# Transposes in place of identity products in a gather that runs beside a recurrent convolution

## The chip, the core and the metric

The kernel runs on one core of a Trainium2 chip. The core has engines that run side by side, each with its own queue of instructions that it works off in order: PE (TensorE, matrix products; its weight loads are listed apart as PEld), DVE (VectorE), ACT (ScalarE) and POOL (GpSimd). SP issues most of the DMAs, POOL the gathers. PE writes to PSUM[...] and the other engines read its results there. The metric is the device time in microseconds (us) of one execution; the median of several runs is given.

## The reference

The input is `x`, 8 images of 128 channels by 64 x 64 points, in fp32. Four layers follow each other, and each adds to its input what it computes from a group-normalized copy (`_gn`). Layer 0 is a selective state-space scan beside a small convolution. Layer 1 is a recurrence: four sweeps over the image (down, up, right, left), in each of which a line becomes itself plus the ReLU of a nine-tap convolution of the line before:

```
def step(prev, cur):
    new = cur + jax.nn.relu(_conv1d(prev, w))
    return (new, new)
```

Layer 2 multiplies a vertical convolution by grouped sums. Layer 3 is a deformable convolution. From an ordinary convolution it takes, for each point and each of nine taps, a position and a mask; it fetches the four corners of the input around the position, sums them with bilinear weights, and multiplies the nine sums by `dcn_w`:

```
samp = corner(y0, x0, ...) + corner(y0, x0 + 1, ...) + corner(y0 + 1, x0, ...) + corner(y0 + 1, x0 + 1, ...)
samp = samp * mask[:, None]
out = jnp.einsum('bckhw,ock->bohw', samp, dcn_w.reshape(COUT, C, KK))
```

A normalization over the batch, gamma and beta, and a leaky ReLU end it.

## The kernel before

Layer 1 works on four images at once, which lie in the tile `X`. Its first four images run beside Layer 0 (`Layer1First`). Its second four run in the main loop of `conv_preact_kernel`, beside Layer 2 and Layer 3 of the first images. The change concerns this main loop.

The loop counts ticks `n`, 96 to an image. In each tick it records, in this order: one step of Layer 1 if one is due (`next(step)`, line 130), which puts the nine products of a line into `ps_l` (L733); the tick of Layer 3 (`three.tick`, line 132) for the image before the one that Layer 2 works on; then the second half of Layer 1's step (line 134), a vector operation that adds the ReLU of `ps_l` to the line in `X` (L741); then what Layer 2's plan has for that tick. The plan (`Layer2.plan`) gives each of its parts a tick by hand: convolution products into `ps_t` (L894, L908), normalization, token transposes that fill the gather tables (`tokens`, L966, which turns 128 x 128 blocks of `x3h` into `ps_tok` by `nc.tensor.transpose`), offset products into `ps_off` (L990), and the positions, masks and weights of the corners on the vector engine (L1023 to L1052). The order in which instructions are recorded is the order in which each engine works; there is no scheduler that would move them. The next step's products need the line that L741 has just written, so PE may have to wait there; what was recorded between the two fills that time.

A tick of Layer 3 handles 128 points and three of the nine taps (`gather`). POOL issues three indirect DMAs (L1123), one per tap, that bring for each point the four corners (four rows of 128 channels) into `got`, or, from tick 402 on, into a part of `X`, which is free by then. `got` has six buffers. The corners 2 and 3 are weighted on ACT (L1134), the corners 0 and 1 on DVE (L1139, into `prod`). What follows depends on `halves`. Line 132 passes 1 while `n < L1Z`, which is 362, and 2 after that. With `halves == 2`, one vector addition (L1141) leaves two partial sums in `got`, and PE adds them. With `halves == 1`, as long as Layer 1 runs, DVE adds all four corners (L1143 to L1145) and leaves one sum, in `got[:, k, 0, :]`.

The sums have points on partitions and channels along the row; the convolution needs channels on partitions. So one tick later `turn` lets PE turn them: for each of the three taps a product with `got` as the stationary operand and the identity as the moving one goes into a third of the PSUM tile `ps_s` (L1155), and with two halves a second product accumulates onto it. Another tick later ACT copies `ps_s` to `samp` (L1106, where `later` calls it), and for each two blocks of points `convolve` multiplies by `dcn_w` into `ps_o` (L1166). `ps_s` has two buffers. `later` runs its calls from `tick`, after that tick's `gather`.

Of the kernel before, what the change touches and what calls it, by code (L numbers as in the profile page):

```python
# [1085 lines left out]
class Layer3:  # L1086
# [63 lines left out]
    def turn(self, halves, got, samp, col):  # L1150
        nc = self.nc
        ps = self.pp.tile([P, self.G3, P], F32, name="ps_s")
        for k in range(self.G3):
            for q in range(halves):
                nc.tensor.matmul(  # L1155
                    ps[:, k, :], lhsT=got[:, k, q, :], rhs=self.ident, start=(q == 0), stop=(q == halves - 1)
                )
        self.later(1, nc.scalar.copy, samp[:, :, col : col + P], ps)

    def convolve(self, b, t0, k0, samp):  # L1160
# [118 lines left out]
```

## Time and profile before

| what | value |
|---|---|
| median of 3 runs | 7738.29 us (7735.23 to 7739.29) |
| the profiled execution | 7708.51 us |
| its span, first to last instruction | 7706.8 us |
| mean granted clock of PE | 0.903 |
| PE busy | 6228.2 us, 81% of the span |
| DVE, POOL, ACT busy | 4497.4, 4009.0, 3460.5 us |
| last product of Layer 1 | 5224 us after the span's start |

Busy time is the union of an engine's instructions. Matmuls are pipelined, so that the duration of one includes a latency that overlaps with the next, and the distance between starts says what one costs in a row of them. The granted clock is the share of full speed that the throttle allows PE. A wait is put down to the last of its releasers that the records name; "issue" and "another core or an unknown queue" stand for releasers that they do not name.

### The profile page before, as it was taken

Reading aid. Unit: us, or ns where it says so; the run is one execution under the profiler, and the core shown is the slowest. Engines: PE = TensorE matmul, PEld = TensorE weight load, DVE = VectorE, ACT = ScalarE, POOL = GpSimd, SP = SyncE. Lnnn points to the kernel's source line nnn. Section 1 sums busy time; section 2 is a strip of 40 time slices with the busy share of each in tenths; the row PEclk is TensorE's granted clock in tenths of the full one; section 3 lists DMA queues with packets and bytes.
Section 4 is the critical chain, followed back from the end, with each engine's and each line's share of the span. In section 5 each row is a group of like instructions: output and inputs, shape, how many; then the busy total and the mean of one; then the engine's idle time right before and its main releaser. Section 6 shows DMA issues by size and latency. Waiting matters only on the chain.

```text
span 7706.8 us, 87506 instructions
## 1 busy us (share of the span) xinstructions
PE 6228.2 (81%) x30574; PEld 4062.3 (53%) x30574; DVE 4497.4 (58%) x5332; ACT 3460.5 (45%) x8218; POOL 4009.0 (52%) x3261
## 2 busy tenths in 40 slices
PE   6888878799999999859898898986678777776661
PEld 1222222255555556637677777775555555555550
DVE  4888889666566566141265666657545454555445
ACT  4555656433333332020155445455455555555552
POOL 3767777444444444000155555456566666666664
PEclk9988889699999999979999999998889888988785
DMA  1011111000000000041255556567666666666667
GB/s 43 27 38 36 39 34 38 31 11 27 12 29 21 9 15 15 12 157 29 66 182 183 166 174 192 167 186 253 204 210 202 208 194 208 201 206 203 186 185 264
DMA packets 333017, 897.81 MB, mean 116 GB/s; under 512 B 55464, under 2 KB 90544, under 8 KB 330528
## 3 DMA queue, kind: packets, MB, share of 16 engines
q0 software_dynamic: 184320, 604.13, 26.0%
q1 hardware_dynamic: 143648, 271.31, 10.6%
q10 hardware_dynamic: 4608, 16.78, 0.5%
q8 instruction: 242, 3.96, 0.2%
q14 instruction: 199, 1.63, 0.1%
HBM read 770.80 MB, written 121.21 MB: 116 GB/s over the span
## 4 chain that ended last, share of the span: by engine, by line
PE 62%; ACT 12%; DVE 8%; issue 8%; another core or an unknown queue 5%; DMA 3%; POOL 2%; SPq 0%; DVEq 0%; POOLq 0%; ACTq 0%
PE u_ps L733 13%; PE ps_l L733 10%; PE ps_s L1155 8%; PE ps_o L1166 6%; PE u_ps L568 5%; ACT X L1134 4%; PE ps_c L477 3%; PE ps_t L894 3%; DVE hb L603 3%; PE ps_y L622 3%; PE ps_x L395 3%; PE ps_t L908 2%; ACT samp L1106 1%; PE ps_off L990 1%
## 5 line engine op out<-in xcount | busy, mean ns | idle before, releaser
L614 POOL TENSOR_TENSOR hb<-hb,bc 128x1024 f32<-128x1024 f32 x512 | 1217.2, 2385 | 1279.7 <-ACT carry L609 893.5
L1123 POOL DMA_INDIRECT X<-table,idx x1386 | 1315.4, 949 | 788.4 <-issue 304.4
L1123 POOL DMA_INDIRECT got<-table,idx x918 | 878.6, 957 | 1351.4 <-DVE idx L1046 545.9
L603 DVE TENSOR_TENSOR_SCAN hb<-da,carry,u_ps 128x512 f32<-128x512 f32 x896 | 1097.8, 1266 | 251.0 <-PE ps_y L622 178.5
L585 ACT ACTIVATE da<-dt_ps 128x1024 f32<-128x1024 f32 x512 | 524.3, 1024 | 1337.7 <-PE dt_ps L568 1337.0
L1155 PE MATMUL ps_s<-ident,X 128*128 128x128 f32 x5544 | 829.7, 308 | 268.0 <-issue 175.7
L1141 DVE TENSOR_TENSOR X<-prod,X 128x768 f32<-128x768 f32 x462 | 442.4, 958 | 916.7 <-ACT X L1134 706.6
L1155 PEld LDWEIGHTS ps_s<-ident,X 128*128 128x128 f32 x5544 | 794.6, 221 | 339.3 <-issue 212.2
L1134 ACT ACTIVATE X<-X,wgt 128x128 f32<-128x128 f32 x2772 | 860.5, 394 | 0.0
L1166 PE MATMUL ps_o<-samp,dcn_w 128*128 128x256 f32 x2304 | 646.3, 422 | 225.3 <-ACT samp L1106 140.5
L568 PE MATMUL u_ps<-u,m_u 32*128 32x512 f32 x2048 | 629.6, 693 | 152.7 <-DVE hb L603 152.5
L1106 ACT COPY samp<-ps_s 128x384 f32<-128x384 f32 x768 | 360.9, 470 | 796.7 <-remote 479.9
L592 DVE TENSOR_TENSOR u_ps<-u_ps,bc 128x1024 f32<-128x1024 f32 x512 | 624.7, 1220 | 153.8 <-PE dt_ps L568 136.9
L568 PE MATMUL dt_ps<-dt,m_dt 32*128 32x512 f32 x2048 | 631.6, 695 | 17.5 <-ACT da L585 17.4
L1166 PEld LDWEIGHTS ps_o<-samp,dcn_w 128*128 128x128 f32 x2304 | 464.6, 212 | 332.9 <-ACT samp L1106 159.6
L1134 ACT ACTIVATE got<-got,wgt 128x128 f32<-128x128 f32 x1836 | 569.5, 393 | 0.0
L1139 DVE TENSOR_TENSOR prod<-X,prod 128x768 f32<-128x768 f32 x462 | 443.6, 960 | 100.6 <-ACT prod L1113 47.1
L741 DVE SCALAR_TENSOR_TENSOR X<-ps_l,X 128x256 f32<-128x256 f32 x252 | 106.2, 421 | 620.3 <-PE ps_l L733 473.4
L568 PEld LDWEIGHTS u_ps<-u,m_u 32*128 32x128 f32 x2048 | 164.8, 196 | 510.0 <-DVE hb L603 311.1
L741 DVE SCALAR_TENSOR_TENSOR X<-u_ps,X 128x256 f32<-128x256 f32 x252 | 106.9, 424 | 501.7 <-PE u_ps L733 501.3
L894 PE MATMUL ps_t<-xn,w 128*128 128x512 f32 (+4 forms) x688 | 305.2, 592 | 54.8 <-ACT t L901 22.5
L1155 PE MATMUL ps_s<-ident,got 128*128 128x128 f32 x2076 | 294.0, 287 | 38.2 <-issue 28.6
(227 smaller groups left out, 10393.2 us busy)
## 6 DMA issues: line engine op xcount, KB each, us to landing
table<-tok SPq DMA_DIRECT2D x128, 256.0 KB
x<-x1d SPq DMA_DIRECT2D x96, 256.0 KB
X<-table,idx POOLq DMA_INDIRECT x1386
x<-x2d SPq DMA_DIRECT2D x48, 384.0 KB
x3h<-x3d SPq DMA_DIRECT2D x16, 1056.0 KB
x_st<-in_x SPq DMA_DIRECT2D x64, 256.0 KB
x_o<-in_x SPq DMA_DIRECT2D x64, 256.0 KB
x1d<-res SPq DMA_DIRECT2D x64, 256.0 KB
```

Of the source, the lines that this page charges most:

```text
L568: nc.tensor.matmul(ps[:, j, :], lhsT=mask[q, r].rearrange("p d n -> p (d n)"), rhs=S[c][src, h][q, :], start=True, stop=True,)
L585: nc.scalar.activation(da, steps[i]["dt"], AF.Exp)
L592: nc.vector.tensor_mul(st["bc"], st["bc"], s["bc", h][:, 0].unsqueeze(1).to_broadcast([P, 2, T]))
L603: nc.vector.tensor_tensor_scan(hb[:, j, :], st["da"][:, j, :], st["bc"][:, j, :], start, ALU.mult, ALU.add)
L614: nc.gpsimd.tensor_mul(hb, hb, S[c]["bc", h][:, 1].unsqueeze(1).to_broadcast([P, 2, T]))
L733: nc.tensor.matmul(ps[:, c0:c1, :], lhsT=w[:, k, :], rhs=v[:, prev, c0 + k - PAD : c1 + k - PAD, :], start=(k == PAD), stop=(k == K - 1),)
L894: nc.tensor.matmul(ps[:, o0 - a0 : o1 - a0, :], lhsT=self.w1[:, k, :], rhs=S["xn", g][:, i0 + o0 : i0 + o1, :], start=(k == 2), stop=(k == 4),
L1123: nc.gpsimd.indirect_dma_start(out=got[:, k, :, :].rearrange("p q c -> p (q c)"), out_offset=None, in_=tab, in_offset=bass.IndirectOffsetO ...
L1134: nc.scalar.activation(got[:, k, q, :], got[:, k, q, :], AF.Identity, scale=wgt[:, t, k0 + k, q : q + 1])
L1139: nc.vector.tensor_mul(prod, got[:, :, 0:2, :], w.unsqueeze(3).to_broadcast([P, G3, 2, C]))
L1155: nc.tensor.matmul(ps[:, k, :], lhsT=got[:, k, q, :], rhs=self.ident, start=(q == 0), stop=(q == halves - 1))
L1166: nc.tensor.matmul(ps, lhsT=self.dcn_w[:, k, :], rhs=samp[:, k - k0, :], start=(k == 0), stop=(k == KK - 1))
```

## The change

In `turn`, where one half is left, each tap's product with the identity is replaced by a PE transpose of the same tile, again with `got` stationary and the identity moving, into the same third of `ps_s`. Where two halves are left, the two accumulating products stay as they are. No other line is touched.

```diff
         for k in range(self.G3):
-            for q in range(halves):
-                nc.tensor.matmul(
-                    ps[:, k, :], lhsT=got[:, k, q, :], rhs=self.ident, start=(q == 0), stop=(q == halves - 1)
-                )
+            if halves == 1:
+                nc.tensor.transpose(ps[:, k, :], got[:, k, 0, :], self.ident)
+                continue
+            for q in range(2):
+                nc.tensor.matmul(ps[:, k, :], lhsT=got[:, k, q, :], rhs=self.ident, start=(q == 0), stop=(q == 1))
         self.later(1, nc.scalar.copy, samp[:, :, col : col + P], ps)
```

## The prediction

> **What bounds the kernel now.** I began with the page: its first part, and the row of the operation that the change touches.
>
> ```profile
> PE 6228.2 (81%) x30574; PEld 4062.3 (53%) x30574; DVE 4497.4 (58%) x5332; ACT 3460.5 (45%) x8218; POOL 4009.0 (52%) x3261
> L1155 PE MATMUL ps_s<-ident,got 128*128 128x128 f32 x2076 | 294.0, 287 | 38.2 <-issue 28.6
> ```
>
> TensorE is the busiest engine over the span, but an average over stages decides nothing. The row counts matmul instructions whose stationary tile is `got`. Line 1123 issues 918 gathers into `got`, three a tick, so 306 ticks. With a of them at `halves == 1`, 2076 = 6a + 12(306 - a) gives a = 266: a fp32 product is recorded as two instructions, six for the three products of a tick. The loop agrees: ticks 96 to 361. The other 40 use `got` with two halves; the 5544 rows on `X` are two halves too. By the starts of `ps_s`, the 266 ticks fill 3821 to 5228 us. The stages by windows (window; busy us and count of PE, PEld, DVE, ACT, POOL; granted clock, DMA share, GB/s):
>
> ```profile
> 3821.00:5228.00 1407.00, 1286.30 (x6549) 1061.21 (x6548) 867.85 (x1438) 709.97 (x2106) 753.09 (x793) 0.97 0.58 178
> 5228.00:5443.00 215.00, 146.67 (x705) 116.64 (x705) 159.96 (x220) 106.76 (x324) 127.09 (x128) 0.82 0.77 254
> 5443.00:7535.00 2092.00, 1482.99 (x8268) 1212.67 (x8267) 1030.70 (x1200) 1172.52 (x3572) 1296.50 (x1367) 0.85 0.65 198
> ```
>
> In the stage of the change PE is busy 91%, the next engine (DVE) 62%; only there does the diff alter an instruction. Then the chain of work that ended last, cut to that window, by line:
>
> ```profile
> by line: PE ps_l L733 36.7%; PE ps_o L1166 9.4%; PE ps_s L1155 8.0%; PE ps_t L894 7.1%; another core or an unknown queue 6.8%; issue 5.4%; PE ps_t L908 3.9%; ACT got L1134 3.4%; PE ps_off L990 2.8%; DVE prod L1139 2.4%; DMA got<-table,idx 1
> ```
>
> `ps_s` holds 8.0% of 1407 us, 113 us of the critical chain. Last, PE's own waits there (us in total, times, longest):
>
> ```profile
> PE ps_l L733 <- DVE X L741: 46.4, 20, 7.8
> PE ps_tok L966 <- ACT tok L969: 27.0, 22, 6.0
> PE ps_l L733 <- issue: 13.2, 9, 4.6
> PE gn_ps L750 <- DVE gn_mv L749: 8.3, 3, 4.1
> ```
>
> PE idles 1407 - 1286 = 121 us, mostly where layer 1's next step waits for the vector add of the last (L741). These waits take part of any gain.
>
> **What the skill says.** "TensorE: Matmul & The Clock Gate", Terms, says the load and the matmul gained a transpose mode on trn2, four times as fast for fp32. Part 4 of that page gives about 275 ns for one transpose in a kernel, and says that transposes do not count as busy for the clock gate. Part 1 says that the gate halves the clock after an idle window of about 3.4 us. The trace already has transposes of this very shape and type, at L966, so their price is measured here (groups of `ps_tok`, then of `ps_s`; ns min/median/max):
>
> ```profile
> L966 PEld LDWEIGHTS ps_tok<-ident,x3h x512: 137/141/231, 3560.5 to 7015.3; 128*128 128x128 f32 x171
> L966 PE MATMUL ps_tok<-ident,x3h x512: 269/273/477, 3560.7 to 7015.4; 128*128 128x128 f32 x171
> L1155 PEld LDWEIGHTS ps_s<-ident,got x2076: 186/192/338, 3821.3 to 5442.1; 128*128 128x128 f32 x189
> ```
>
> 512 rows are 64 calls of eight: one instruction each. 273 ns agrees with the page's 275. It is latency, though; what counts is the spacing, in PE's timeline:
>
> ```profile
> 4098.94 0.83 PE L1155 MATMUL ps_s<-ident,got 128*128 128x128 f32 x6
> 4099.61 0.60 PE L966 MATMUL ps_tok<-ident,x3h 128*128 128x128 f32 x4
> ...
> 4102.72 0.83 PE L1155 MATMUL ps_s<-ident,got 128*128 128x128 f32 x6
> 4103.39 0.80 PE L733 MATMUL ps_l<-X,w_up 128*128 128x256 f32 x3
> ```
>
> Six product instructions take 0.67 us to the next group's start, 0.111 each, 0.223 a product. Four transposes span 0.60 with the last one's 0.273: (0.60 - 0.27) / 3 = 0.109 each. So the trace shows a factor of two, not the page's four. Following `ps_s` directly, they show no cost of switching mode.
>
> **The change, part by part.**
> 1. Removed: 266 x 6 = 1596 matmul instructions and their weight loads. Added: 266 x 3 = 798 of each. A tick's turn falls from 0.67 to 3 x 0.109 = 0.33 us, saving 0.34; 266 x 0.34 = 90 us of PE time. The loads (192 ns before, 141 then) run beside the matmuls and are not summed.
> 2. What of it is on the path. All turns cost 266 x 0.67 = 178 us; 113 lie on the chain, 63%. Of these 0.34/0.67 = 51% goes: 57 us. The other turns stand under a wait. Layer 1's 173 steps in the timeline say the same: in 48 the next step's products start within 0.08 us of the vector add's end, so PE waited, and 57 of the 266 turns lie in such steps. There nothing is gained; if the remaining 209 all counted, 71 us. I take 57, since the chain also sees stretches where DVE sets the pace through several steps. From 4700 to 4830 it adds Layer 2's positions and weights (L1023 to L1052) to the gather's sums, and PE's savings pile up in front of the next add.
> 3. New waits. In 15 further steps PE's margin over the add is under the turns' saving: 1 us lost in all. Longer idles can call the half clock: 16 such spells, 85 us together, lie in the stage, 5.3 us each, so one costs at most half, 2.7 us. For two more I charge 5 us, an estimate; both ends are zero and six (16 us).
> 4. Nothing is moved. Order on all queues, tiles, the bank, waits before each product and DMAs stay. The scalar copy of `ps_s` (L1106) can start 0.34 us earlier, `got` is free earlier, and POOL may issue the next gathers earlier; with POOL at 54% and DMA at 0.58 busy I cost that at nothing. If gathers were late instead, the vector product L1139 would be late next, then the add L741 behind it in DVE's queue, then PE; the saving of each such tick would be gone. After 5228 all work is unchanged and starts earlier.
>
> Sum: 57 - 1 - 5 = 51 us. The profiled execution took 7708.5 us (span 7706.8), so 7657.5 would be its like. The median of the runs, 7738.3, lies 29.8 above it; I carry that over: 7738.3 - 51 = 7687.3, said as 7687.
>
> **The rivals.** (a) PE sets nearly everything: only the turns under PE's visible waits are lost, 71 us, 7667; 80 with some waits caused by PE itself, 7658. For it: 91% busy, and 12.2% of the chain is "issue" or unknown, where PE work may hide. Against it: the runs of DVE work in the chain. (b) The waits absorb it: faster PE meets DVE and ACT, as in 4700 to 4830 all along; 8 us remain, 7730. For it: 121 us of idle and queues that stand still in order. Against it: DVE has 539 us idle in the stage, and between 3821 and 4000 PE is busy 176.35 of 179 us. (c) Slower: the transposes starve the clock gate, as the page's remark allows. The place is this stage, the price PE's remaining 1286 - 90 = 1196 us at 0.97: a clock c costs 1196 x (0.97/c - 1). It eats the 57 us below c = 0.926; at 0.90 it costs 93, net 36 slower, 7774. Against it: each step keeps 18 true products (3.75 us) and the trace's transposes at 4099 us run amid a full-clock stretch. (d) The transposes cost as much as products, no change, 7738: against it stands L966.
>
> **How the numbers follow.** Chances: 0.61 for 51 us (own range 7670 to 7705: the end costs of part 3, and 10 us either way for the unnamed chain pieces), 0.20 for (a), 0.10 for (b), 0.07 for (c), 0.02 for (d). From 7654 to 7716 lie nearly all of the first (0.59), most of (a) (0.18) and a little of (b) (0.03): 0.80. A measurement of this kernel tells about 0.2%, 15.5 us, from no change. Faster by more: 0.60 of the first, all of (a), 0.04 of (b), 0.84. Within: 0.01 + 0.06 + 0.02, 0.09. Slower: (c), 0.07.
>
> **What would show it.** Step 1: 798 transposes at L1155 in place of 1596 products, `ps_s` on `got` down from 2076 to 1278 instructions, three transposes spaced 0.109 us, next group 0.33 us after the first. Step 2: the stage from the first gather turn to the end of layer 1 near 1356 instead of 1407 us, DVE busy unchanged near 868. Step 3: PE's idle up from 121 to about 160 us (1356 less 1196), clock 0.96 to 0.97. Step 4: from layer 1's end to the program's end the same length within 5 us. I am wrong if the transposes are spaced above 0.2 us, if the clock of the stage falls below 0.93, or if PE's idle grows by 80 us or more. A stage shorter by over 65 us would say that the chain's unnamed pieces were PE's.

## The result

| | before | changed |
|---|---|---|
| median of 6 runs, us | 7738.79 (7735.23 to 7742.24) | 7683.34 (7673.36 to 7704.86) |
| profiled execution, us | 7708.51 | 7673.36 |
| first gather turn to layer 1's last product, us | 1402.7 | 1375.0 |
| from there to the end of the span, us | 2482.5 | 2477.9 |

The ratio is 0.9933, 95% interval 0.9921 to 0.9944: 55 us faster by the medians, where 51 was forecast. The interval is 43 to 61 us. The two profiled executions differ by 35 us only; that of the kernel before lies 27 us under its lowest timed run.

What the change did to the instructions is in the groups of `ps_s` of the changed kernel (ns min/median/max, first and last start):

```profile
L1155 PEld LDWEIGHTS ps_s<-ident,got x798: 138/141/370, 3818.5 to 5196.9; 128*128 128x128 f32 x200
L1155 PE MATMUL ps_s<-ident,got x798: 270/273/454, 3818.7 to 5197.0; 128*128 128x128 f32 x200
L1158 PE MATMUL ps_s<-ident,got x480: 272/275/582, 5197.1 to 5409.9; 128*128 128x128 f32 x160
```

798 + 480 = 1278 product and transpose instructions on `got` in place of 2076; the 40 ticks with two halves (L1158) are as they were. Their spacing, in PE's timeline of the changed kernel:

```profile
4091.45 0.49 PE L1155 MATMUL ps_s<-ident,got 128*128 128x128 f32 x3
4091.78 0.60 PE L966 MATMUL ps_tok<-ident,x3h 128*128 128x128 f32 x4
...
4094.89 0.49 PE L1155 MATMUL ps_s<-ident,got 128*128 128x128 f32 x3
4095.21 3.92 PE L733 MATMUL ps_l<-X,w_up 128*128 128x256 f32 x18
```

A turn costs 0.33 us to the next group, as forecast (the median over the 266 turns is 0.328 us, 0.668 before), and nothing is added where PE goes from transposes back to products. Now the stages of the changed kernel (window; busy us and count of PE, PEld, DVE, ACT, POOL; clock, DMA share, GB/s):

```profile
3818.50:5197.00 1378.50, 1213.70 (x5751) 964.33 (x5750) 867.42 (x1436) 706.36 (x2105) 750.09 (x793) 0.96 0.59 182
5197.00:5411.00 214.00, 145.54 (x704) 115.83 (x703) 159.69 (x220) 106.93 (x324) 126.38 (x128) 0.82 0.77 254
5411.00:7504.00 2093.00, 1490.48 (x8268) 1221.04 (x8267) 1031.87 (x1201) 1173.67 (x3572) 1294.17 (x1367) 0.85 0.65 198
```

Only the first stage is shorter. In it PE's busy time fell from 1286 to 1214 us, and its idle time rose from 121 to 165. Its waits there (us in total, times, longest):

```profile
PE ps_l L733 <- DVE X L741: 69.5, 28, 8.8
PE ps_tok L966 <- ACT tok L969: 21.1, 20, 4.9
PE ps_l L733 <- issue: 15.9, 19, 2.2
PE ps_tok L966 <- issue: 14.9, 4, 8.2
```

The wait for layer 1's addition grew from 46 to 70 us, which is 23 of the 44 us of new idle time. The busy time fell by 72 us and not by the 90 that the turns save. Most of the difference lies in layer 1's own products, which follow these waits (windows of `ps_l`, before and changed; the stage's length, then busy us and count of PE, PEld, DVE and ACT, clock, DMA share, GB/s):

```profile
3821.00:5228.00 1407.00, 711.34 (x3118) 600.40 (x3116) 73.06 (x174) 0.00 (x0) 0.97 0.58 178
3818.50:5197.00 1378.50, 723.75 (x3116) 607.82 (x3114) 73.28 (x174) 0.00 (x0) 0.96 0.59 182
```

They take 12 us longer, while the clock's record has 27 us more at half speed in the stage. On the chain of work that ended last, cut to this stage, `ps_s` has 4.0% in place of 8.0%, and "issue" has 9.4% in place of 5.4%:

```profile
by line: PE ps_l L733 34.8%; issue 9.4%; PE ps_o L1167 8.8%; PE ps_t L894 6.8%; another core or an unknown queue 5.8%; PE ps_s L1155 4.0%; ACT got L1134 3.8%; PE ps_t L908 3.7%; DVE prod L1139 3.2%; PE ps_off L990 2.8%; DVE got L1144 2.4%; 
```

### The profile page after: what moved, and what is told of

Its sections match the earlier page's. It is cut to its first block, busy times and chain, and to the rows that moved or that the text cites. A ratio compares the mean times of both kernels' runs of the same rounds, so it can differ in the third digit from the quotient of the medians.

```text
span 7671.6 us, 85910 instructions
## 1 busy us (share of the span) xinstructions
PE 6160.0 (80%) x29776; PEld 3972.6 (52%) x29776; DVE 4496.0 (59%) x5332; ACT 3459.2 (45%) x8218; POOL 4000.2 (52%) x3261
## 3 DMA queue, kind: packets, MB, share of 16 engines
q1 hardware_dynamic: 143648, 271.31, 10.7%
## 4 chain that ended last, share of the span: by engine, by line
PE 60%; ACT 11%; DVE 10%; issue 9%; another core or an unknown queue 5%; DMA 3%; POOL 2%; SPq 0%; DVEq 0%; POOLq 0%; ACTq 0%
PE u_ps L733 13%; PE ps_l L733 10%; PE ps_s L1158 7%; PE ps_o L1167 5%; PE u_ps L568 5%; ACT X L1134 4%; PE ps_c L477 3%; PE ps_t L894 3%; DVE hb L603 3%; PE ps_y L622 3%; PE ps_x L395 2%; PE ps_off L990 1%; PE ps_t L908 1%; ACT samp L1106 1%
## 5 line engine op out<-in xcount | busy, mean ns | idle before, releaser
L1158 PE MATMUL ps_s<-ident,X 128*128 128x128 f32 x5544 | 834.7, 310 | 266.5 <-issue 166.2
L1158 PEld LDWEIGHTS ps_s<-ident,X 128*128 128x128 f32 x5544 | 802.6, 223 | 337.7 <-issue 197.9
L622 PE MATMUL ps_y<-hb,m_y 128*32 128x512 f32 x2048 | 312.9, 665 | 3.4 <-POOL hb L614 3.1
```

The costliest lines, as they stand in the source:

```text
L622: nc.tensor.matmul(S[c]["ps_y", h][32 * j : 32 * j + 32, :], lhsT=m_y[:, r, :], rhs=steps[i + j // 2]["hb"][:, j % 2, :], start=(r == 0), ...
L1158: nc.tensor.matmul(ps[:, k, :], lhsT=got[:, k, q, :], rhs=self.ident, start=(q == 0), stop=(q == 1))
```

## The experiments

The theory: the gain is PE time of the turns that no wait covers, and waits behind DVE and ACT absorb the rest. The rivals: nearly all of the turns' time counts; the clock gate, which grants PE a lower clock where it works little (0.76 against 0.95 in e10 and e12), takes part of it back, because transposes don't count as work; something other than PE time made the gain. The twelve runs fell on three chips, which ran the kernel before in two different times: 7740 us on the one of e1 to e4, called the slower chip here, and 7217 us on that of e5 to e8 and on that of e9 to e12, the faster chips. The result above has the slower time; its chip isn't recorded. Each run is compared with the kernel before on its own chip; the last part of this section tells what the difference between them shows.

**The changed kernel again.** No edit.

> The changed kernel once more, as it stands, on the chip of the next three runs. All theories expect the ratio near 0.993 again (7683 us beside 7739). What it tells is the spread: the six runs of the changed kernel spanned 31 us, those of the kernel before 7 us. If the spread comes from the chip or the moment, the changed kernel's runs lie within 10 us here; if from its own waits, they spread by 20 to 30 us again.

It took 7694.79 us (six runs from 7670.97 to 7697.7) beside 7739.86, ratio 0.9937 (0.9922 to 0.9952). The spread of 27 us returned on one chip, with five of the six runs within 5 us of each other. But the 19 runs of the kernel before beside it spread by 32 us, from 7725 to 7757, so the spread tells nothing of the changed kernel's own waits. Its profiled execution took 7693.78 us, close to its median.

**Each transpose twice.**

```diff
-                nc.tensor.transpose(ps[:, k, :], got[:, k, 0, :], self.ident)
+                for _ in range(2):
+                    nc.tensor.transpose(ps[:, k, :], got[:, k, 0, :], self.ident)
```

> Each transpose is issued twice into the same place, so a turn costs PE 6 x 0.109 = 0.65 us, as much as the products' 0.67, but all of it in transposes. Theory (the gain is PE time of the turns on the path, nothing else): the time of the kernel before within 10 us, 7729 to 7749, and a granted clock of 0.97 in the stage. Rival (transposes starve the clock gate): at least 30 us slower than before, with the stage's clock below 0.95. Rival (something other than PE time made the gain, say the loads or the earlier copy): at least half of the gain stays, under 7712.

7736.78 us beside 7739.86, ratio 0.9996 (0.9987 to 1.0006): the gain is gone once PE's time is as long as before. So it was the time that a turn takes on PE, and neither the shorter loads nor anything else about transposes. The run puts the end of a turn back too, so it doesn't separate PE's time from the earlier start of the copy `samp`; PE hardly waits for these copies, since its waits in the stage before have none of `ps_o` and 0.2 us of `ps_s`. The stage, in windows:

```profile
3817.50:5249.00 1431.50, 1287.43 (x6540) 1044.78 (x6539) 867.24 (x1436) 708.66 (x2103) 751.62 (x792) 0.96 0.57 175
```

With PE busy as long as before the change (1287 against 1286 us), this stage is 25 us longer than in the first profile of the kernel before. The clock of 0.96 is 0.01 under the expected one and above the rival's 0.95.

**Each product twice**, in the ticks of one half:

```diff
-                nc.tensor.transpose(ps[:, k, :], got[:, k, 0, :], self.ident)
+                for _ in range(2):
+                    nc.tensor.matmul(ps[:, k, :], lhsT=got[:, k, 0, :], rhs=self.ident, start=True, stop=True)
```

> Products as before the change, each issued twice into the same place in the ticks of one half: 266 x 0.67 = 178 us of PE time more than the kernel before. Theory (PE sets the stage for about two thirds of its turns, and longer PE work covers waits): slower by at least 63% of that, 112 us, and at most 178; 7850 to 7917. Rival (waits on DVE and ACT set the stage, PE is covered): slower by under 60 us, under 7800.

7819.29 us, ratio 1.0105 (1.0084 to 1.0126): 79 us for 178 us of PE time, 45%, between the two expectations. The stage shows what took the rest:

```profile
3817.00:5324.00 1507.00, 1437.44 (x8130) 1222.92 (x8129) 868.40 (x1437) 710.96 (x2104) 749.53 (x792) 0.99 0.55 167
```

Against the run above the stage grew by 75.5 us and PE's busy time by 150; 74.5 us of idle was filled (144.1 to 69.6). And the clock rose from 0.96 to 0.99: its record has 34 us at half speed in the stage, where the run above has 102. So the added work bought some of its own time back, as longer work left fewer idle stretches.

**One half everywhere**, so transposes after layer 1 too:

```diff
-                three.tick(b, i, two.done[b], 1 if n < L1Z else 2, n >= L1R)
+                three.tick(b, i, two.done[b], 1, n >= L1R)
```

> On top of the change, one half and transposes also in the 502 ticks after layer 1: a turn there falls from twelve product instructions (1.34 us) to three transposes (0.33), 1.0 x 502 = 502 us of PE time less, and DVE does three additions of 0.57 us in place of one of 0.96, 0.75 x 502 = 377 us more. In the stage from 5443 to 7535 the chain has 23.7% of 2092 us, 496 us, on these products. Theory (where PE is on the chain its time counts): three quarters of 496 us goes at most, 370; with new waits behind DVE and ACT I expect 150 to 300 us less than the changed kernel, 7380 to 7530. Rival (after layer 1 the weights on ACT and the gathers set the pace): within 40 us of the changed kernel or slower than it.

7673.85 us, ratio 0.9918 (0.9902 to 0.9934), 21 us under the changed kernel on that chip; the theory's 150 to 300 us did not come, and the rival's forecast, within 40 us, held. The stage after the switch to `X`:

```profile
5405.00:7494.00 2089.00, 1114.38 (x4137) 706.67 (x4138) 1384.71 (x2155) 1173.56 (x3595) 1312.70 (x1382) 0.72 0.66 201
```

PE is busy for 1114 us in place of 1490, and the stage has its length, 2089 against 2093. The 24% that `ps_s` has on the chain there brought nothing. But DVE is busy for 1385 us in place of 1032, so this run alone doesn't say what PE's time was worth. The clock fell from 0.85 to 0.72, which e11 and e12 take up.

> One half and transposes everywhere, once more. Where the gathers are issued without a break, three of them take POOL 3 x (0.95 + 0.30) = 3.75 us a tick, and 462 ticks take 1733 us: that is the 1731 us that the stage after the switch to X took on the chip of the last four runs with nothing changed there. Theory (the gathers set that stage, PE's turns do not): within 15 us of the changed kernel on either chip, the stage still 1731 or 2090. Rival (PE sets it where releases are on time): at least 60 us faster than the changed kernel.

The same kernel on a faster chip took 7213.52 us, ratio 0.9996 (0.9988 to 1.0005), 49 us more than the changed kernel there. The theory's band of 15 us is missed on that side; the rival's gain did not come either.

**The kernel before again**, the first run on a faster chip.

> The kernel before, unchanged, profiled once more. Its first profiled execution took 7708.5 us where its 19 timed runs beside the last experiments lie between 7725 and 7758. Theory: that execution was a lucky one, and a second one takes about 7739 with a stage from the first gather turn to layer 1's last product of 1425 to 1440 us in place of 1403, as in the run with each transpose twice (1429). Rival: profiled executions of this kernel are faster than timed ones by some 30 us, then this one takes about 7709 again, with 1403 in the stage.

7218.15 us beside 7216.89. Its profiled execution took 7220.33 us, so the rival, that profiled executions are some 30 us faster than timed ones, fails here. Whether 7708.5 was a lucky execution of the slower chip could not be answered on this one. The run showed something else, told at the end of this section. Its stage, in windows:

```profile
3809.00:5112.00 1303.00, 1253.85 (x6525) 1040.00 (x6524) 862.51 (x1432) 708.07 (x2103) 751.99 (x792) 0.99 0.63 192
```

PE is busy for 1254 us of it and idle for 49. The chain of work that ended last, cut to it, and PE's waits:

```profile
by line: PE ps_l L733 44.6%; PE ps_o L1166 11.4%; PE ps_s L1155 10.7%; PE ps_t L894 7.6%; PE ps_t L908 4.5%; issue 3.4%; PE ps_off L990 3.0%; DMA got<-table,idx 2.4%; ACT got L1134 2.2%; PE ps_tok L966 1.9%; ACT tok L969 1.1%; DVE prod L113
PE ps_l L733 <- DVE X L741: 16.9, 13, 2.5
PE ps_tok L966 <- ACT tok L969: 16.7, 24, 0.7
```

**The early and the late ticks alone.** `turned` is set in the main loop and asked for in `turn`; the other turns of one half keep the product. The edit of the early ticks, against the changed kernel, with lines left out at `...`; the late ones have `>= 33`:

```diff
+            three.turned = (n - 1) % N < 33
...
+            if halves == 1 and self.turned:
+                nc.tensor.transpose(ps[:, k, :], got[:, k, 0, :], self.ident)
+                continue
             if halves == 1:
-                nc.tensor.transpose(ps[:, k, :], got[:, k, 0, :], self.ident)
+                nc.tensor.matmul(ps[:, k, :], lhsT=got[:, k, 0, :], rhs=self.ident, start=True, stop=True)
                 continue
```

> Transposes only in the turns of each image's first 33 gather ticks (99 of the 266); the other 167 keep the product. In the first profile the chain runs through 78% of the instructions of these turns. Theory: 99 x 0.34 x 0.78 = 26 us faster than before, less a few us for half clock: 15 to 30. Rival (only the total of PE work counts, not its place): 99/266 of the change's 52, 19 us.

> The other part alone: transposes in the 167 turns after each image's first 33 ticks, where layer 2 adds tokens, offsets, positions and weights. The chain runs through 52% of these turns. Theory: 167 x 0.34 x 0.52 = 30 us faster, less the half clock: 18 to 30, per turn two thirds of what the early ones bring. Rival (place doesn't matter): 167/266 of 52, 33 us. Rival (the vector engine sets these ticks): under 10 us.

Early: 7193.9 us, 23.0 us less than before, ratio 0.9966 (0.9952 to 0.9979). Late: 7193.33 us, 23.6 less, 0.9969 (0.9957 to 0.9981). A turn brings 23.0/99 = 0.23 us in the early ticks, 68% of the 0.34 that it saves, and 23.6/167 = 0.14 us in the late ones, 41%. By the intervals that is 0.15 to 0.35 us a turn early and 0.08 to 0.19 late. The two overlap, so that the place matters is likely and not shown. Of the rival that the place does not matter, the 19 us for the early part lie within the interval, and the 33 us for the late part lie just beyond it (14 to 31 us). The other rival of the late ticks, under 10 us, is out.

**The addition ahead of the gather.** Layer 1's addition, which stood behind the tick's gather sums in DVE's queue, is recorded ahead of them:

```diff
+            if l1:
+                next(step)
             if b >= 0:
                 three.tick(b, i, two.done[b], 1 if n < L1Z else 2, n >= L1R)
-            if l1:
-                next(step)
```

> The changed kernel with layer 1's addition (L741) recorded ahead of the tick of layer 3, so that on the vector engine it stands before that tick's gather sums and not behind them. In the changed kernel PE idles 165 us in the stage, of which its waits put some 90 on this addition and on gather sums. Theory (these waits are what absorbed the rest of the gain): the addition starts within 0.1 us of the products' end, PE's idle falls by 50 us or more, and the time by 30 to 70, to 7620 to 7660. Rival (the vector engine's work has to be done anyway, and its gather sums, now late, hold PE's next turn): within 15 us of the changed kernel, or slower.

7297.86 us, ratio 1.0113 (1.0097 to 1.0128): 81 us slower than before, and 133 us slower than the changed kernel on the other faster chip. The addition does start within 0.1 us of the products' end, and PE hardly waits for it any more. But the sums now start after it, PE stands at the turns, and DVE stands at the addition (PE's waits in the stage):

```profile
PE ps_s L1155 <- issue: 65.4, 29, 3.4
PE ps_s L1155 <- ACT got L1134: 34.3, 14, 3.0
PE ps_l L733 <- DVE X L741: 5.3, 28, 0.2
```

The line of DVE among the waits of all engines:

```profile
DVE X L741 <- PE ps_l L733: 410.9, 155, 8.2
```

DVE now stands idle for 411 us while PE makes the line's products, where in the changed kernel of e9 it is 157 us; it used to make sums in that time. The rival was right: these waits can't be had by exchanging the two.

**The changed kernel on a faster chip.**

> The changed kernel as it stands, beside the kernel before. On the chip of the last four runs the kernel before took 7217 us, and the two partial edits 23.0 and 23.6 us less. Theory (the turns' savings add up, wherever they stand): 47 us less than before on that chip, ratio 0.9935; where the kernel before takes 7739, 52 us less, 0.993. Rival (with its releases on time that chip has PE busy 96% of the stage, so that the whole gives more than the parts): 60 to 85 us less there, ratio 0.988 to 0.9915.

7164.67 us beside 7216.36, ratio 0.993 (0.9916 to 0.9943): 51.7 us less. The parts gave 23.0 + 23.6 = 46.6, so they add up within the intervals, and the rival's 60 to 85 us is out by the median and at the edge of the interval (60.6 us). Its stage, in windows:

```profile
3818.00:5076.00 1258.00, 1180.73 (x5752) 944.28 (x5750) 864.75 (x1436) 705.67 (x2105) 753.14 (x793) 0.99 0.66 200
```

and PE's waits in it:

```profile
PE ps_l L733 <- DVE X L741: 36.1, 34, 3.2
PE ps_tok L966 <- ACT tok L969: 16.7, 24, 0.7
```

PE's busy time fell by 73 us (1253.85 to 1180.73), its idle rose by 28 (49 to 77), 19 of them at the addition, and 45 us arrived. Counted to layer 1's last product the stage is 48 us shorter. The time at half speed in it rose from 20.5 to 37.5 us.

**Do transposes count for the clock gate?** Two kernels like one half everywhere, which differ from it in `turn` after layer 1 alone: one product a tap, and each transpose four times. The edit of the second, against the changed kernel, with lines left out at `...`; the first has one `nc.tensor.matmul` in place of the loop:

```diff
+            three.layer1 = n <= L1Z
...
-                three.tick(b, i, two.done[b], 1 if n < L1Z else 2, n >= L1R)
+                three.tick(b, i, two.done[b], 1, n >= L1R)
...
+            if self.layer1:
+                nc.tensor.transpose(ps[:, k, :], got[:, k, 0, :], self.ident)
+                continue
             if halves == 1:
-                nc.tensor.transpose(ps[:, k, :], got[:, k, 0, :], self.ident)
+                for _ in range(4):
+                    nc.tensor.transpose(ps[:, k, :], got[:, k, 0, :], self.ident)
                 continue
```

> As one half everywhere, but with one product a tap in place of one transpose in the ticks after layer 1: 0.67 us of products a turn, where one half everywhere has 0.33 us of transposes and the changed kernel 1.34 us of products. Read for the granted clock in the stage after the switch to X, which was 0.85 in the changed kernel and 0.72 with one half everywhere. Theory (the gate goes by how long PE works, whatever the work): between those two. Rival (transposes do not count as work for the gate): close to the changed kernel's, since every turn has true products.

> As one half everywhere, but each transpose issued four times into the same place in the ticks after layer 1: 12 x 0.109 = 1.31 us of transposes a turn, as long as the changed kernel's twelve product instructions there. Theory (the gate goes by how long PE works): the clock of the changed kernel in that stage, within 0.03. Rival (transposes do not count): the clock of one half everywhere, or below it.

They took 7218.56 and 7211.53 us, in one execution each. The stage after the switch to `X` in windows, on the same chip, first one half everywhere:

```profile
5270.00:7031.00 1761.00, 1070.83 (x4136) 676.26 (x4136) 1383.09 (x2153) 1191.09 (x3596) 1311.09 (x1381) 0.76 0.78 238
```

with one product a tap:

```profile
5280.00:7046.00 1766.00, 1221.22 (x5534) 901.89 (x5535) 1384.85 (x2156) 1188.99 (x3596) 1311.76 (x1382) 0.80 0.78 238
```

and with four transposes a tap:

```profile
5275.00:7037.00 1762.00, 1351.40 (x8324) 1049.61 (x8325) 1384.24 (x2154) 1190.27 (x3596) 1308.40 (x1382) 0.95 0.78 238
```

The changed kernel has 0.94 there. With 0.33, 0.67 and 1.31 us of PE work a turn the clock is 0.76, 0.80 and 0.95: in these runs it goes by how long PE works, and four transposes hold it as well as the changed kernel's products (1.34 us a turn, 0.94). The remark in the Trainium skill, "TensorE: Matmul & The Clock Gate", Part 4, that a transpose doesn't count as busy in the same way, does not hold in these runs.

The three lengths, 1761, 1766 and 1762 us, are equal with PE busy from 1071 to 1351 us: with DVE's three sums a tick PE doesn't set this stage. The changed kernel, with one sum a tick and as much PE work as the third (1354 us), has 1726 us; so the sums and not PE's time cost the 36 us (one execution each). What POOL waited for says how (first two lines the changed kernel, the third one half everywhere):

```profile
POOL X L1123 <- issue: 148.7, 487, 0.5
POOL X L1123 <- ACT X L1134: 30.5, 100, 0.3
POOL X L1123 <- ACT X L1134: 78.9, 233, 4.0
```

In the changed kernel no gather starts more than 0.5 us after the end of the one before: POOL issues them without a break, 0.95 us each and 0.30 between two, which makes 1733 us for the stage's 462 ticks (the window has 1370 of their 1386 gathers) and so sets the length, although `ps_s` has 11.6% of the chain there. With one half everywhere single gathers wait up to 4.0 us for ACT's weighting. How the sums hold up ACT was not followed, and no run has less PE work after layer 1 without DVE's longer sums; on the slower chip, where the gathers are not issued without a break, PE's share there stays untested.

**What the chips showed.** In the first profile of the kernel before, many instructions of the stage start late with no releaser in the records, some of them microseconds after the end of the matmuls that they needed. The view of waits calls these "remote" (us, times, longest):

```profile
ACT samp L1106 <- remote: 92.2, 31, 7.0
DVE X L741 <- remote: 67.7, 17, 6.9
```

Engines release each other by semaphores. On the faster chip of e5 the same program has no such wait in the stage. There the record of PE's semaphore updates follows the matmul's end by 13 ns nearly always; in the stage of the first profile 32% of the matmuls that signal have no such record within 0.3 us of their end. Records may be missing there, but the late starts are real: 43 of the stage's 173 additions of layer 1 start over 0.1 us after the last product's end with DVE idle, 103 us in sum (44 and 102 us in the changed kernel), and none does in e5 or e9. As the sums before and after are the same, these late additions are no part of the gain. The stage of the kernel before took 1403 us there and 1303 in e5, and from layer 1's end to the last turn it took 2308 and 1935 us. What delays the releases was not tried.

## Why the prediction was right

Step 1 was right to the microsecond: 798 transposes, 0.33 us a turn, and by windows of the tile 126.75 us of PE for `ps_s` in the stage in place of 216.75, 90.0 less. The 275 ns with which it found its 273 in agreement is, in the Trainium skill, "TensorE: Matmul & The Clock Gate", Part 4, a figure given for a bf16 transpose; these are fp32.

Step 2 was right in its size for the medians: it put 57 us on the path, and 55 came, 45 in e1 and 52 on a faster chip, after the losses of step 3. Its 63% as a measure was not confirmed. By ticks the chain of the first profile has 78% early and 52% late, and the runs gave 68% and 41%, after the same losses. But on the faster chip, where these two ran, the chain of the kernel before has 10.7% of 1303 us, 139 us, on `ps_s`, which is 78% of all turns' time. Reckoned as in step 2, that would be 71 us, and 52 came; the half clock, half of 17 us more, does not make up the difference. So the chain's share was a bound from above there.

Step 3 had the idle right (165 us against "about 160") and the clock of 0.96, but the half clock too small. Not two spells were added but five (113 us at half speed in place of 85), and in the second run of the changed kernel seven (126 us); at half their length, as the step reckons, that is 14 to 20 us and not 5. That is most of what is missing where PE's busy time fell by 72 us and not by 90, and it shows as the 12 us more of layer 1's products. The rest is small; part of it is that the 0.27 us of a turn's last transpose count as busy whether PE has work in them or not. How long PE must stand idle for a spell was not measured.

Step 4 was right: the rest of the program has its length within 5 us (2482.5, 2477.9).

The sum was right for the medians and not for the execution that it was made against. The stage was to be near 1356 us and took 1378.5: 18 us more of PE's busy time and 5 more of idle. Carrying over the 29.8 us between the first profiled execution and the median was the weakest step: 7708.5 lay below every timed run beside it, whereas the profiled executions of the changed kernel and of e1 to e4 lay within 11 us of their medians. So the changed kernel's first one should have been 7657, and was 7673.4. That the kernel before had a fast execution there is what the stage of e2 suggests (1431.5 us with the same PE time), but it was not repeated on that chip. That the median was met within 4 us, with the stage missed by 22, is in part luck.

The rivals: (a) fell where it had its best case, with PE busy 96% of the stage before the change: 51.7 us, not 71. (b) holds in part, as the 28 to 44 us of new idle show. (c) fell by e2 and e12; the 18 true products a step that it speaks of are nine, recorded as 18 instructions. (d) fell by the first timeline. None of the prediction's signs of being wrong appeared. The 63% must not be read as a law: in e3 79 us came of 178.

## What to carry to other kernels

An fp32 product with the identity that only turns a tile, with nothing to accumulate, is better a transpose: 0.109 us in place of 0.223 for 128 x 128. What of that arrives depends on what waits behind it, here 45 to 55 of 90 us. An edit that pays the time back without the benefit (each transpose twice) tells in one run whether the gain is the time of that instruction. A share of the chain of waits is a first bound and no price: after layer 1 on the faster chip the gathers' issue sets the length, and the chain still runs through `ps_s` for 11.6%.

## What was not expected of the hardware

The same program took 7740 us on one chip and 7217 on two others, with consumers that started late in the gather's stages on the first. In the gather's stage the granted clock offset part of each edit of PE's work: 68 us less at half speed where PE had 150 us more to do (e3 against e2), and 27 to 41 us more on the slower chip, 17 on the faster one, where it had 72 or 73 less. Transposes hold the clock as products do (0.95 and 0.94). And the factor of four that the Trainium skill gives for fp32 transposes, "TensorE: Matmul & The Clock Gate", Terms, without saying against what, was two against the two-instruction product here, 0.223 to 0.109 us.
